# A graph-attention layer and a graph convolution on one core: new order of the first loads and products, adjacency transposed on VectorE, shorter sums and another order at the end

## The chip, the cores and the metric

The kernel runs on one core of one Trainium2 chip. The metric is the device time of one execution in microseconds (us). The numbers come from repeated executions and from one execution taken with the hardware profiler, whose trace has the start and the duration of every instruction. Times in the trace count from its first instruction; the time from there to the last one is called the span. An engine name in a profile line means: PE is TensorE (matrix products), PEld its loading of the stationary operand, DVE is VectorE, ACT is ScalarE, POOL is GpSimd, SP is SyncE (which here issues all loads and stores).

## The reference

There are 32 items x of 512 rows and 512 columns (fp32), one 512x512 adjacency of zeros and ones, three weights Wq, Wk, Wv with biases, and one weight W1 with bias b1.

```python
q, k, v = x @ Wq + bq, x @ Wk + bk, x @ Wv + bv          # 8 heads of 64
scores = einsum('bihd,bjhd->bhij', q, k) / 8 + where(adj == 0, -1e9, 0)
x = layernorm(x + softmax(scores) @ v)
y = einsum('nm,bmd->bnd', adj, x)
x = layernorm(x + y @ W1 + b1)
```

## The kernel before

**Products.** A product of two 512x512 matrices is made by seven products of 256x256 blocks instead of eight (a scheme of Strassen's kind). FACTORS (L53) names the two factors of each of them. Products 1 (A11 with B11) and 2 (A12 with B21) need plain blocks; the other five need sums and differences of blocks, such as S1 = A21 + A22, S2 = S1 - A11 and T1 = B12 - B11. A is the transposed item (tile xT, seven slots), B the weight (tiles wq, wk, wv, w, seven slots). The tile of a slot is overwritten where it can be: S3 takes the place of A21, T3 that of B12. `sum_weights` (L299) makes one sum of a weight on VectorE, `combine_rows` (L311) those of an item. `block_product` (L343) makes one of the seven, four matmuls into one of eight PSUM banks; since the data are fp32 the trace shows two records for each matmul, here called passes. `project` (L353) makes a product for q, k or v and adds it from the bank to its places.

**An item's way.** An item comes in as blocks or squares, and is transposed. q, k and v are made. The scores are products of k and q for a pair of heads at a time (L558); VectorE adds the mask (`gap`, one byte per element, 1 where the adjacency is zero) while it takes them out of PSUM (L560); ScalarE makes the exponentials (L562); GpSimd adds them up (L573); `attend` (L575) multiplies them with v (L582). `fold_squares` (L609) transposes the added exponentials in squares of 32, sums them, and sends the parts through HBM to their rows (`passed`, L626 and L633). `add_up` (L635) makes the sums and their reciprocals of a group of four heads, and also keeps running totals of both (`sums`, L639; `inverses`, L641), from which `judge` (L668) decides at the end whether the scheme was safe for these data; if not, a plain kernel would run. `scale_rows` and `add_rows` (L647, L654) add the attention to the item. Then come the layer norm (`statistics`, `square_root`, `invert_root`, `normalise`, L406 to L428), the splitting of each normalised item into a high part, exact in the faster matmul type, and the low rest (`split_high`, `split_low`, L430 to L443; L443 also adds b1 to the item on GpSimd), the product with the adjacency (`aggregate`, L462), the seven products with W1 (`convolve`, L513), the second norm and the store.

**Order.** The order is written out by hand; nothing reorders it. Each engine does its instructions in the order of the program. The items are staggered: while item b is in attention, b+1 is projected and b-1 aggregated and convolved. `units_of` (L756) lays these units between the products. Loads and stores all go through SyncE's queue in program order, with eight semaphores used in turn, so that a DMA waits until the one eight places before it has landed.

**The start.** L260 and L261 load item 0 in four blocks of 128 rows and Wq in two halves of its columns. `x_transpose` (L317) transposes a block by four matmuls with the identity into one bank; ScalarE copies the bank (L326), and for the two lower blocks VectorE adds S1 (L328). The first loads after that, from Wk on, wait for a small write to `wk` by ScalarE (L695) that stands behind the third block's copy. The adjacency is loaded whole (L700), and its four block rows are transposed on TensorE (L284) between products of k and v; `adjacency` (L281) then copies the bank (ScalarE, L285) and compares it (VectorE, L286).

**The end.** In the last group there are no more scores. `last_residual` (L658) transposes the attention of the last two pairs of heads on TensorE, multiplies by the reciprocals (L663) and adds to the last item (L665). Its norm, its splitting by rows (`split_rows`, L478) and its aggregation (`aggregate_rows`, L494, with 32 matmuls at L501) follow; beside them the item before it gets its seven products (`rest`), b1 is added (`add_bias`, L491), `judge` runs, and the last item's seven products (`last`) begin when L506 and L508 have copied the banks. The four 128-row blocks of the last item are normalised and stored one by one.

Of the kernel before, what the change touches and what calls it, by code (L numbers as in the profile page):

```python
# [207 lines left out]
def fast_kernel(ctx: ExitStack, tc, verdict, x, adj, Wq, bq, Wk, bk, Wv, bv, W1, b1, out):  # L208
# [28 lines left out]
    def load_blocks(b):  # L237

        for c in range(NB):
            IN[b, c] = work.tile([P, D], FP, name="xin", bufs=XIN)  # L240
            nc.sync.dma_start(IN[b, c], x[b, c * P:(c + 1) * P, :])

    def load_squares(b):


        for d in range(DB):
            IN[b, d] = work.tile([P, N // SQ, SQ], FP, name="xin", bufs=XIN)
            for i in range(P // SQ):
                cols = x[b, :, d * P + i * SQ:d * P + (i + 1) * SQ]
                nc.sync.dma_start(IN[b, d][i * SQ:(i + 1) * SQ, :, :], cols.rearrange("(j r) f -> r j f", r=SQ))  # L250
# [9 lines left out]
    load_blocks(0)  # L260
    wq = load_factors(Wq, "wq")  # L261
# [9 lines left out]
    sums = consts.tile([P, NB, GROUP], FP, name="sums")  # L271
    inverses = consts.tile([P, NB, GROUP], FP, name="inverses")
    nc.gpsimd.memset(sums, 0.0)
    nc.gpsimd.memset(inverses, 0.0)
# [6 lines left out]
    def adjacency(c):  # L281
        pt = bank(NB, P)
        for m in range(NB):
            nc.tensor.transpose(pt[:, m, :], adj_s[:, c, m * P:(m + 1) * P], ident)  # L284
        nc.scalar.activation(adjT[:, :, c * P:(c + 1) * P], pt, AF.Copy)  # L285
        nc.vector.tensor_scalar(gap[:, :, c * P:(c + 1) * P], pt, 0.0, None, op0=ALU.is_equal)  # L286

    def look_for_low_half(c):

        kept = work.tile([P, N], FR, name="high")  # L290
        nc.scalar.activation(kept, adj_s[:, c, :], AF.Copy)
        cut = work.tile([P, N], FP, name="attT")
        nc.vector.tensor_tensor(cut, adj_s[:, c, :], kept.bitcast(FP), op=ALU.not_equal)
# [23 lines left out]
    def x_transpose(b, c):  # L317

        if c == 0:
# [3 lines left out]
        for d in range(DB):  # L323
            nc.tensor.transpose(pt[:, d // 2, d % 2, :], IN[b, c][:, d * P:(d + 1) * P], ident)
        below, cols = c // 2, slice(c % 2 * P, (c % 2 + 1) * P)
        nc.scalar.activation(xt[:, 2 * below:2 * below + 2, :, cols], pt, AF.Copy)  # L326
# [16 lines left out]
    def block_product(pm, t, w, i, turned=False):  # L343
# [4 lines left out]
        for r in range(2):  # L348
# [4 lines left out]
    def project(b, which, i):  # L353
# [12 lines left out]
        pm = bank(2, half)  # L366
        block_product(pm, XT[b], w, i, turned=not values)
# [19 lines left out]
    def flips(b):  # L387

        return [(turn_squares if b else x_transpose, b, c) for c in range(NB)] + [(sum_rows, b)] if b < B else []
# [538 lines left out]
```

## Time and profile before

| What | us |
|---|---|
| median of three executions | 2744.57 (2743.18 to 2746.03) |
| profiled execution, its own time | 2743.55 |
| its span in the trace | 2741.7 |
| TensorE busy within the span | 2720.6 |
| VectorE, ScalarE, GpSimd busy | 2145.6, 1411.0, 1914.2 |
| first product with a weight begins | 8.30 |
| first scores begin | 38.34 |
| last product with a weight ends | 2729.53 |

A line of the timeline gives the start, the duration, the engine, the source line, the operation, what it writes and reads, the shape, and how many such instructions were merged; in brackets stands how long the engine was idle before it, and what ended that. The idle time of an engine costs something only if the engine, or one that waits for it, is what the end waits for.

### The profile page before, as it was taken

How to read it: one execution, taken by the hardware profiler on the slowest of the kernel's cores; microseconds unless marked ns; L12 is line 12 of the kernel's file. 1: busy time of each engine (PE TensorE's matmuls, PEld its weight loads, DVE VectorE, ACT ScalarE, POOL GpSimd, SP SyncE). 2: the span in 40 equal slices, each digit the busy share in tenths (PEclk: the TensorE clock that was granted, in tenths of full speed). 3: DMA queues.
4: the chain of work that ended last, by engine and by line, in shares of the span. 5: the costliest groups of instructions: out<-in, count | busy, mean ns of one | idle time of the engine just before them, and what ended most of it. 6: DMA issues, size and time to landing. Idle time of an engine off the chain costs nothing.

```text
span 2741.7 us, 36328 instructions
## 1 busy us (share of the span) xinstructions
PE 2720.6 (99%) x12344; PEld 1903.7 (69%) x12344; DVE 2145.6 (78%) x3540; ACT 1411.0 (51%) x2459; POOL 1914.2 (70%) x1221
## 2 busy tenths in 40 slices
PE   9999999999999999999999999999999999999997
PEld 6676676766766767667677676676776766767765
DVE  6878778788787787877877778778778787787787
ACT  3455464555544655545545455464465544655554
POOL 4776677766867667777677766686766867767774
PEclk9999999999999999999999999999999999999998
DMA  5223231233221332212323123331233222332121
GB/s 159 49 36 79 69 74 36 60 79 75 67 44 56 75 79 63 54 51 71 79 67 63 45 64 79 71 71 39 61 76 77 65 48 55 72 79 64 48 63 48
DMA packets 632927, 179.16 MB, mean 65 GB/s; under 512 B 578464, under 2 KB 582560, under 8 KB 632736
## 3 DMA queue, kind: packets, MB, share of 16 engines
q1 hardware_dynamic: 632736, 176.79, 27.3%
q8 instruction: 99, 1.62, 0.2%
q14 instruction: 92, 0.75, 0.1%
HBM read 108.01 MB, written 68.68 MB: 64 GB/s over the span
## 4 chain that ended last, share of the span: by engine, by line
PE 96%; DVE 2%; DMA 0%; ACT 0%; POOL 0%; issue 0%; SPq 0%; DVEq 0%; ACTq 0%
PE bank L350 56%; PE bank L558 17%; PE bank L582 16%; PE bank L469 8%; DVE bnst L412 0%; DVE e L560 0%; DMA wq<-in_L_gnn_Wq_dram 0%; DVE xs L531 0%; DVE xT L531 0%; DVE k L442 0%; POOL xs L529 0%; ACT xs L427 0%; DVE sums L639 0%; DVE stat L413 0%; DVE part L861 0%
## 5 line engine op out<-in xcount | busy, mean ns | idle before, releaser
L562 ACT ACTIVATE e<-e 128x1024 f32<-128x1024 f32 x512 | 524.9, 1053 | 575.2 <-DVE e L560 539.9
L573 POOL TENSOR_TENSOR es<-e 128x1024 f32<-128x1024 f32 x128 | 316.5, 2473 | 481.1 <-ACT e L562 481.1
L560 DVE SCALAR_TENSOR_TENSOR e<-gap,bank 128x512 f32<-128x512 uint8 x1024 | 617.7, 678 | 20.2 <-PE bank L558 20.2
L573 POOL TENSOR_TENSOR es<-es,e 128x1024 f32<-128x1024 f32 x256 | 618.9, 2418 | 20.1
L558 PE MATMUL bank<-q,k 64*128 64x512 f32 x2048 | 463.7, 598 | 0.0
L582 PE MATMUL bank<-e,v 128*64 128x512 f32 x2048 | 453.6, 595 | 0.0
L350 PE MATMUL bank<-wv,xT 128*128 128x256 f32 x1792 | 405.4, 381 | 0.0
L350 PE MATMUL bank<-xT,wk 128*128 128x256 f32 x1792 | 402.8, 379 | 0.0
L350 PE MATMUL bank<-xT,wq 128*128 128x256 f32 x1792 | 400.8, 381 | 1.2 <-DMA wq<-in_L_gnn_Wq_dram 1.0
L350 PE MATMUL bank<-w,yT 128*128 128x256 f32 x1792 | 392.6, 379 | 2.7 <-DVE yT L506 2.7
L350 PEld LDWEIGHTS bank<-wv,xT 128*128 128x128 f32 x1792 | 337.7, 190 | 70.2 <-DVE e L560 24.3
L350 PEld LDWEIGHTS bank<-xT,wq 128*128 128x128 f32 x1792 | 337.8, 190 | 69.9 <-DVE e L560 23.5
L558 PEld LDWEIGHTS bank<-q,k 64*128 64x128 f32 x2048 | 203.8, 186 | 258.3 <-issue 147.8
L350 PEld LDWEIGHTS bank<-w,yT 128*128 128x128 f32 x1792 | 340.1, 190 | 51.4 <-DVE yT L506 3.1
L350 PEld LDWEIGHTS bank<-xT,wk 128*128 128x128 f32 x1792 | 340.2, 190 | 46.1
L652 ACT ACTIVATE rows<-rows,zero,inverse 128x64 f32<-128x64 f32 x1008 | 343.1, 426 | 2.1 <-DVE inverse L640 2.1
L582 PEld LDWEIGHTS bank<-e,v 128*64 128x64 f32 x2048 | 141.3, 137 | 277.1 <-issue 275.7
L562 ACT ACT_TABLE_LOAD x30 | 38.5, 1283 | 406.1 <-DVE e L560 406.1
L442 DVE TENSOR_TENSOR low<-xs,high 128x512 fp32r<-128x512 f32 x122 | 163.1, 1337 | 61.5 <-ACT high L438 61.5
L531 DVE TENSOR_TENSOR xs<-bank,xs 128x512 f32<-128x512 f32 x186 | 124.3, 683 | 96.6 <-PE bank L350 57.2
L427 ACT ACTIVATE xs<-xs,shift,rstd 128x512 f32<-128x512 f32 x248 | 181.9, 803 | 32.0 <-DVE shift L422 21.3
L443 POOL TENSOR_TENSOR xs<-xs,b_r 128x512 f32<-128x512 f32 x124 | 157.4, 1282 | 21.5 <-DVE low L442 21.5
(125 smaller groups left out, 3013.0 us busy)
## 6 DMA issues: line engine op xcount, KB each, us to landing
turned<-attT SPq DMA_DIRECT2D x126, 256.0 KB, 2.0
rows<-turned SPq DMA_DIRECT2D x504, 64.0 KB, 2.5
xin<-in_x_dram SPq DMA_DIRECT2D x496, 64.0 KB, 2.4
xs<-in_x_dram SPq DMA_DIRECT2D x31, 1024.0 KB, 5.2
out_dram<-xs SPq DMA_DIRECT2D x31, 1024.0 KB, 4.4
part<-passed SPq DMA_DIRECT2D x256, 8.0 KB, 1.8
passed<-part SPq DMA_DIRECT2D x64, 32.0 KB, 1.5
xin<-in_x_dram SPq DMA_DIRECT2D x4, 256.0 KB, 3.2
```

The source lines that it names most:

```text
L350: nc.tensor.matmul(pm[:, r, :], left[:, d, r * P:(r + 1) * P], right[:, d, :], start=(d == 0), stop=(d == 1))
L427: nc.scalar.activation(row, row, AF.Identity, bias=SHIFT[t][:, slot:slot + 1], scale=RSTD[t][:, slot:slot + 1])
L442: nc.vector.tensor_sub(LOW[b, d], cols, HIGH[b, d].bitcast(FP))
L443: nc.gpsimd.tensor_add(cols, cols, b1_r[:, None, d * P:(d + 1) * P].to_broadcast([P, NB, P]))
L469: nc.tensor.matmul(pm.rearrange("p a n -> p (a n)"), part, adjT[:, n % NB, :], start=(n == 0), stop=(n == 2 * NB - 1))
L531: nc.vector.tensor_add(block, pm, block)
L558: nc.tensor.matmul(ps[s], keys[:, j * P:(j + 1) * P], queries, start=True, stop=True)
L560: nc.vector.scalar_tensor_tensor(e[:, s, :], gap[:, j, :], NEG * root, ps[s], op0=ALU.mult, op1=ALU.add)
L562: nc.scalar.activation(e, e, AF.Exp, scale=1.0 / root)
L573: nc.gpsimd.tensor_add(ES[b, hp], ES[b, hp] if j > 1 else E[b, hp, 0], E[b, hp, j])
L582: nc.tensor.matmul(po[s * HD:(s + 1) * HD, :], values, e[:, s, :], start=(j == 0), stop=(j == NB - 1))
L652: nc.scalar.activation(part, part, AF.Identity, bias=zero, scale=inverse[:, c, s:s + 1])
```

## The change

It has these parts.

1. Item 0 and Wq are loaded in smaller pieces in another order: left halves of the first two blocks, B11, their right halves, the two lower blocks, B21, B12, B22. TensorE transposes the left halves, makes half of product 1, transposes the right halves, makes the other half, transposes block 2 and block 3, and makes product 2, before the five products that need sums. What is added from the banks of products 1 and 2 keeps its place in the order of the adding.
2. The adjacency is loaded in 16 pieces, placed so that VectorE's transposition of 32x32 squares gives the transposed matrix. It is transposed there and not on TensorE. The 16 loads stand behind those of Wv and bv. ScalarE copies and VectorE compares the result from SBUF.
3. `add_up` keeps one running total of both sums and reciprocals, added by GpSimd in one instruction; VectorE's addition goes. `judge` takes one reduction in place of two and a minimum in place of two multiplications.
4. In the last group the second folding and the fetching of its parts come before the last two low parts. For the last item but one b1 is added by `add_bias` after the last item's statistics are issued, and no longer in `split_low`.
5. After the last group the last item's statistics come before the first of the `rest`; the second norm's statistics of the item two places before the last, and the biases of the last item, are laid between the products of `rest`. The last store but one and the last change places.

The numbers of rows and columns computed stay as they were. The core of the diff:

```diff
-    def load_blocks(b):
-        for c in range(NB):
+    def load_block(b, c, cols=slice(0, D)):
+        if (b, c) not in IN:
             IN[b, c] = work.tile([P, D], FP, name="xin", bufs=XIN)
-            nc.sync.dma_start(IN[b, c], x[b, c * P:(c + 1) * P, :])
+        nc.sync.dma_start(IN[b, c][:, cols], x[b, c * P:(c + 1) * P, cols])
...
+    def place_squares(t, rows, d):
+        for i in range(P // SQ):
+            cols = rows[:, d * P + i * SQ:d * P + (i + 1) * SQ]
+            nc.sync.dma_start(t[i * SQ:(i + 1) * SQ, :, :], cols.rearrange("(j r) f -> r j f", r=SQ))
...
-    load_blocks(0)
-    wq = load_factors(Wq, "wq")
+    for c in range(2):
+        load_block(0, c, slice(0, half))
+    load_factor("B11", 0, 0)
+    for c in range(2):
+        load_block(0, c, slice(half, D))
+    for c in (2, 3):
+        load_block(0, c)
+    for name, r, c in (("B21", 1, 0), ("B12", 0, 1), ("B22", 1, 1)):
+        load_factor(name, r, c)
...
     def adjacency(c):
-        pt = bank(NB, P)
-        for m in range(NB):
-            nc.tensor.transpose(pt[:, m, :], adj_s[:, c, m * P:(m + 1) * P], ident)
-        nc.scalar.activation(adjT[:, :, c * P:(c + 1) * P], pt, AF.Copy)
-        nc.vector.tensor_scalar(gap[:, :, c * P:(c + 1) * P], pt, 0.0, None, op0=ALU.is_equal)
+        turned = work.tile([P, N], FP, name="attT")
+        nc.vector.transpose(turned, adj_s[:, c, :, :].rearrange("p j f -> p (j f)"))
+        nc.scalar.activation(adjT[:, c, :], turned, AF.Copy)
+        nc.vector.tensor_scalar(gap[:, c, :], turned, 0.0, None, op0=ALU.is_equal)
...
-    def x_transpose(b, c):
+    def x_transpose(b, c, sides=(0, 1)):
...
-        for d in range(DB):
+        for d in (2 * s + k for s in sides for k in range(2)):
             nc.tensor.transpose(pt[:, d // 2, d % 2, :], IN[b, c][:, d * P:(d + 1) * P], ident)
...
-        nc.gpsimd.tensor_add(cols, cols, b1_r[:, None, d * P:(d + 1) * P].to_broadcast([P, NB, P]))
+        if b != B - 2:
+            nc.gpsimd.tensor_add(cols, cols, b1_r[:, None, d * P:(d + 1) * P].to_broadcast([P, NB, P]))
...
-        nc.vector.tensor_reduce(inverse, PART.pop((b, g)).rearrange("p a c h -> p c h a"), axis=AX.X, op=ALU.add)
-        nc.vector.tensor_add(sums, sums, inverse)
-        nc.vector.reciprocal(inverse, inverse)
-        nc.gpsimd.tensor_add(inverses, inverses, inverse)
+        nc.vector.tensor_reduce(total, PART.pop((b, g)).rearrange("p a c h -> p c h a"), axis=AX.X, op=ALU.add)
+        nc.vector.reciprocal(inverse, total)
+        nc.gpsimd.tensor_add(watched, watched, both)
...
-        nc.vector.tensor_reduce(seen[:, 0:1], sums, axis=AX.XY, op=ALU.add)
-        nc.vector.tensor_reduce(seen[:, 1:2], inverses, axis=AX.XY, op=ALU.add)
+        nc.vector.tensor_reduce(seen[:, 0:2], watched.rearrange("p k c h -> p k (c h)"), axis=AX.X, op=ALU.add)
...
-        nc.vector.tensor_mul(well[:, 0:1], well[:, 0:1], well[:, 1:2])
-        nc.vector.tensor_mul(well[:, 0:1], well[:, 0:1], well[:, 2:3])
+        nc.vector.tensor_reduce(well[:, 3:4], well[:, 0:3], axis=AX.X, op=ALU.min)
...
-    turned, first = flips(0), projections(0)
-    run(turned[:3])
+    first = projections(0)
+    for c in range(2):
+        x_transpose(0, c, (0,))
+    one, two = bank(2, half), bank(2, half)
+    block_product(one, XT[0], wq, 1, turned=True, parts=(0,))
+    for c in range(2):
+        x_transpose(0, c, (1,))
+    block_product(one, XT[0], wq, 1, turned=True, parts=(1,))
+    x_transpose(0, 2)
...
-    adj_s = work.tile([P, NB, N], FP, name="yT", bufs=1)
-    nc.sync.dma_start(adj_s, adj.rearrange("(c p) m -> p c m", p=P))
     wv = load_factors(Wv, "wv")
     bv_r = load_row(nc, consts, bv, "bv_r")
+    adj_s = work.tile([P, NB, N // SQ, SQ], FP, name="yT", bufs=1)
+    for c in range(NB):
+        place_squares(adj_s[:, c, :, :], adj, c)
...
-    run(turned[3:NB])
+    x_transpose(0, 3)
+    block_product(two, XT[0], wq, 2, turned=True)
...
-    run(first[:1])
+    project(0, "q", 1, one)
...
-    run(first[3:5])
+    run(first[3:4])
+    project(0, "q", 2, two)
...
-            behind = [fresh[:2], fresh[2:], young[:1] + scaled[:1], young[1:3], young[3:5] + [first],
-                      young[5:] + splits[:1], splits[1:] + scaled[1:]]
-            return [merge(convolution(b - 2), behind), [second] + fetched + added + gathered]
+            behind = [fresh[:2], fresh[2:], young[:1] + scaled[:1], young[1:3], young[3:5] + [first],
+                      young[5:] + splits[:1], splits[1:2] + [second] + fetched + splits[2:] + scaled[1:]]
+            return [merge(convolution(b - 2), behind), added + gathered]
...
-    run(rest[:1])
     for c in range(NB):
         statistics(t, 0, c)
+    for c in range(NB):
+        add_bias(t - 1, c)
+    run(rest[:1])
     ahead = norm(t, 0)
     run(ahead[:1] + rest[1:2] + ahead[1:2])
+    older, seen = survey(t - 2), survey(t - 1)
     for c in range(NB):
         run(ahead[2 + c:3 + c])
         split_rows(t, c)
+        if c == 0:
+            add_bias(t, c)
+        if c == 2:
+            run(older[:2])
         run(rest[2 + c:3 + c])
-    run(rest[2 + NB:])
-    older, seen = survey(t - 2), survey(t - 1)
-    run(older)
-    for c in range(NB):
-        add_bias(t, c)
+        if c > 0:
+            add_bias(t, c)
+    run(rest[2 + NB:] + older[2:])
     well = judge()
...
-    store(t, [2, 3])
+    store(t, [3, 2])
```

## The prediction

> **What bounds the kernel now.** I read the page's busy table and chain first, then TensorE's waits, then the windows and the timeline at both ends.
>
> ```profile
> PE 2720.6 (99%) x12344; PEld 1903.7 (69%) x12344; DVE 2145.6 (78%) x3540; ACT 1411.0 (51%) x2459; POOL 1914.2 (70%) x1221
> PE 96%; DVE 2%; DMA 0%; ACT 0%; POOL 0%; issue 0%; SPq 0%; DVEq 0%; ACTq 0%
> ```
>
> TensorE is busy in 2720.6 of 2741.7 us. So between the ends nothing but fewer products can help, and the diff leaves those products alone. VectorE work saved there (63 of the 64 additions of L639) is worth nothing. What can be won lies in the 21.1 us in which TensorE is idle, in products that go, and in stretches where it runs slowly. Its waits, in total, times, longest:
>
> ```profile
> PE bank L501 <- DVE low L489: 3.2, 1, 3.2
> PE bank L350 <- DVE yT L506: 2.7, 1, 2.7
> PE bank L690 <- DVE attT L687: 1.1, 1, 1.1
> PE bank L350 <- DMA wq<-in_L_gnn_Wq_dram: 1.0, 1, 1.0
> ```
>
> Two waits are in the last 40 us, two at the start; 12.2 us more lie behind the last product (2729.53 to 2741.7). The windows of TensorE (start:end, length, busy, granted clock, DMA) show a cost that no wait shows:
>
> ```profile
> 2700.00:2704.00 4.00, 0.76 (x4) 0.85 0.00 0
> 2704.00:2708.00 4.00, 4.00 (x10) 0.50 0.01 4
> 2708.00:2712.00 4.00, 4.00 (x15) 0.80 0.00 0
> ```
>
> After the 3.24 us of idling the clock falls to half: L501's products follow each other every 0.43 us until 2709.5, and every 0.24 us after. Two timeline stretches, VectorE at the end and the first products:
>
> ```profile
> 2692.18 0.26 DVE L638 TENSOR_REDUCE inverse<-part 128x16 f32<-128x64 f32 x1 [3.50 <-DMA part<-passed]
> 2692.47 1.09 DVE L639 TENSOR_TENSOR sums<-sums,inverse 128x16 f32<-128x16 f32 x1
> ...
> 2714.24 1.18 DVE L676 TENSOR_TENSOR well<-well 128x1 f32<-128x1 f32 x1
> 2715.45 1.19 DVE L677 TENSOR_TENSOR well<-well 128x1 f32<-128x1 f32 x1
> ```
>
> ```profile
> 7.99 0.42 DVE L328 TENSOR_TENSOR xT<-bank,xT 128x256 f32<-128x256 f32 x1 [0.20 <-ACT xT L326]
> 8.30 1.97 PE L350 MATMUL bank<-xT,wq 128*128 128x256 f32 x8 [0.97 <-DMA wq<-in_L_gnn_Wq_dram]
> 9.75 0.69 DVE L302 TENSOR_TENSOR wq<-wq 128x512 f32<-128x512 f32 x1 [1.33 <-DMA wq<-in_L_gnn_Wq_dram]
> 10.49 7.17 PE L350 MATMUL bank<-xT,wq 128*128 128x256 f32 x32 [0.23 <-DVE wq L302]
> 24.41 0.60 PE L284 MATMUL bank<-ident,yT 128*128 128x128 f32 x4
> ```
>
> A multiplication of one element per partition (L676) takes 1.18 us, on the path to L506 for which TensorE waits.
>
> **What the skill says.** "SBUF — State Buffer", Who interferes with whom: a VectorE instruction with two SBUF inputs and a GpSimd one that reads SBUF exclude each other for the whole instruction. The trace agrees: L676 and L677 end at 2715.42 and 2716.64, near the boundaries of GpSimd's four L492 of 1.24 us each (2711.65 to 2716.62). The same section says that tensor_reduce never contends; L670 to L672 took about 0.15 us beside a running L492. "TensorE: Matmul & The Clock Gate", Part 1: after an idle window of about 3.4 us the clock is halved, and the window runs freely, so the moment varies. The trace agrees with 3.24 us here, while the wait of 2.72 us left the clock at 1.00.
>
> **The start.** All times are on the trace's clock. The data are the same 2 MB; the four x blocks and Wq landed from about 4.0 to 9.7 us, some 0.83 us per 256 KB. By the new order I estimate the two left halves landed by 4.0, B11 by 4.9, right halves 5.7, block 2 by 6.5, block 3 by 7.3, B21 8.1, B12 9.0, B22 9.8. SyncE issues ten instead of six DMAs at 0.45 us, the last near 5.3, so it isn't the limit.
> - Left transposes: 4.21 to 5.06 (0.213 each, half clock as now). Two copies on ScalarE at 4.88 and 5.31; the first half of product 1 starts at 5.83. The clock rose near 6.4 in this trace: two passes at 0.43, two at 0.216, end 7.12.
> - Right transposes to 7.55 (0.108 each), second half of product 1 to 8.41, block 2 to 8.84, block 3 to 9.27, product 2 (eight passes, 1.73) to 11.0.
> - The next product (5) needs S1 and T1. ScalarE copies block 2 at 9.04 and block 3 at 9.66 (its 0.6, and L695 between); VectorE's two L328 end at 10.1 and 10.7, T1 at 11.3, product 5 at 11.37. Today it starts at 10.49: 0.88 later, but product 2 is done: **-0.85**.
> - The new waits: VectorE's T1 queues behind L328 of block 3, with product 5 behind it. The load of Wk waits for L695, now 9.7 instead of 7.23, with all of SyncE's later loads behind it. Wk lands by about 15; its first product is due at 16.5, so this costs nothing. The bank of product 2 stays occupied longer, but the order built from the changed kernel gives it to no product before v's first.
> - The 16 transposes of the adjacency (L284) leave TensorE: from 24.41 to 31.34 are 6.93 us, less three products of 1.73: **-1.75**. Their work goes to VectorE: four transposes at 0.62 (L335's price for 128x512) and four comparisons from SBUF of 0.3 to 0.7, in place of four of 0.68. VectorE has gaps over 1 us between its instructions there.
> - The adjacency now comes in 16 DMAs of 128-byte pieces. Sixteen such loads of x took 14.2 us of SyncE beside other loads (13.57) and 8.7 us alone (77.96). I take 10 us behind Wk, Wv and bv (18.8): last landing 28.8, needed at about 31.2; VectorE can be some 3 us late before the scores (35.7) wait. The loads of x behind them move to about 39, wanted at 56. Cost 0.
>
> **The end.**
> - The second folding moves ahead of the last two low halves (L442). With the bias additions (L443) gone from GpSimd, L442 d=1 runs 2680.2 to 2680.9 (now 1.40), the fold until 2683.3 instead of 2687.45. The part's store and fetch take 4.7 us, so it lands at 2688.1 instead of 2692.2. Low half d=2 is made at 2683.5 to 2684.2, if the lock alternates as now; TensorE wants it at 2683.68. **+0.6** on TensorE (up to 1.9 if both L656 go first); its seven products with W1 for the last item but one then end at about 2701.2 instead of 2700.55.
> - add_up starts after L474 at about 2689.2: reduction 0.29, reciprocal 0.36, no L639, then the four of L663/L665 (2.68) to 2692.55, four statistics (3.2) to 2695.75. GpSimd's four biases stand at 2693.3 to 2698.3. L531 of product 1 waits for two of them (2695.85). L422 has two SBUF inputs: it may be blocked until 2698.3. I take that; unblocked it is 1.0 earlier. ScalarE's normalisation at 2698.45, the first low row at 2700.6 (L427 to PE now takes 2.34). So TensorE has no wait: L501 starts at about 2701.2, at full clock.
> - L501: 32 at 0.235 are 7.5 us; the fourth low row, which I find blocked by GpSimd until 2706.35, costs 0.3: end about 2709.0 instead of 2713.98.
> - VectorE then: two L531, two statistics (2709.7), two reductions, a tensor_scalar that waits for GpSimd (2710.8; L674 did so, 0.55), two short ones: L506 at 2711.1 instead of 2716.56. Products resume at 2711.85 instead of 2717.30: **-5.45**. GpSimd is free by 2712.1, and its L315 starts at about 2713.2.
> - From there the order is the same, until the last stores: block 3 goes out when ready (2735.24), block 2 at 2735.7; today the last is issued at 2736.14: **-0.4**.
> - The middle: **0**. `watched` takes the place of the addition to `inverses` on GpSimd (0.22 for 16 elements; 32 are now added), under a TensorE that never pauses; without that cover, twice 0.22 in 64 groups would cost 14 us at most.
>
> Sum: -0.85 - 1.75 - 5.45 - 0.4 = -8.45. The span goes from 2741.7 to 2733.25, the profiled execution (2743.55) to 2735.1. That execution is 1.02 under the median 2744.57, so I forecast 2736.1.
>
> **Rivals.**
> 1. The front gives nothing. TensorE's work now starts while the clock may still be half; if it rises at 8 instead of 6.4, product 5 is 1.3 later, and the S1 chain hides nothing. Today slack before 8.30 swallows that. Worth 2.1 less: 2738.2. Against it: in this trace the clock had risen by 6.66.
> 2. The locks fall well: L422 and the tensor_scalar aren't blocked, 2 us better: 2734.1.
> 3. The locks fall badly, or the clock halves again while TensorE waits for L506 (2.2 us by my times, under the 2.72 that did no harm). Eight products' passes at half speed for some 3 us and one more block of 1.25: about 3.4 less: 2739.5.
> 4. Slower: the adjacency's small pieces come late. The first scores need its last comparison, 3.1 us after the landing. They start at 38.34 today; break-even (with 5.85 won at the end) is a landing at 41. If the 16 loads take 29 us (1.8 each, twice what the busiest stretch shows), landing is at 48 and the time 2744.57 - 8.45 + 15.4 = 2751.5. The 0.89 seen when crowded gives 33, within slack.
>
> **Chances.** Forecast 0.50, rival 1 0.20, rival 2 0.14, rival 3 0.12, rival 4 0.04. 0.2% (5.5 us) is about what a measurement of this kernel can tell from no change. Faster than 2739.1: the forecast, rival 2, most of rival 1, a little of rival 3: 0.79. Within: 0.16. Slower: 0.05. The range spans rivals 2 to 3, with 1.5 us for the spread of the runs: 2732.6 to 2740.0.
>
> **What would show it.** L284 gone from TensorE; product 5 near 11.4 with product 2 ahead of it; scores near 35.7. TensorE's wait at L501 under 0.5 us and PEclk at 1.0 in 2700 to 2712; add_up near 2689; L506 near 2711; the last product ending near 2721.5 (now 2729.5, less 8.05 of start and end). Wrong if scores wait for VectorE's comparison, if the clock still falls at the end, or if the first sums are ready much after 11.4.

## The result, and the profile after

| What | before, us | after, us |
|---|---|---|
| median | 2744.57 (2743.18 to 2746.49) | 2732.80 (2731.98 to 2734.13) |
| profiled execution: its time, its span | 2743.55, 2741.7 | 2731.98, 2730.2 |
| TensorE, VectorE busy | 2720.6, 2145.6 | 2716.4, 2103.9 |
| k's first product begins | 17.50 | 15.89 |
| first scores begin | 38.34 | 34.98 |
| first scores to the last attend (L582, now L600) | 2633.63 | 2633.23 |
| last attend to the first VectorE copy of the last aggregation (L506, now L524) | 44.59 | 37.39 |
| that copy to the end of the last ScalarE operation (L427, now L444) | 19.12 | 19.20 |
| from there to the end of the span | 6.0 | 5.4 |

The ratio is 0.9957, with a 95% interval of 0.9944 to 0.9970: 11.8 us less, where 8.5 were forecast (2736.1; range 2732.6 to 2740.0). The stretches of the table add up along the path: -3.36 - 0.40 - 7.20 + 0.08 - 0.6 = -11.5, the difference of the spans.

The page's busy line and the engines' shares of its chain of waits, of the kernel after:

```profile
PE 2716.4 (99%) x12328; PEld 1900.3 (70%) x12328; DVE 2103.9 (77%) x3478; ACT 1410.8 (52%) x2461; POOL 1913.8 (70%) x1220
PE 97%; DVE 1%; POOL 0%; DMA 0%; ACT 0%; issue 0%; SPq 0%; DVEq 0%; ACTq 0%; POOLq 0%
```

TensorE has 16 passes fewer, and still bounds all but the ends. Its waits after (us in total, times, longest):

```profile
PE bank L365 <- DVE yT L524: 1.9, 1, 1.9
PE bank L707 <- DVE attT L704: 1.1, 1, 1.1
PE bank L365 <- ACT xT L341: 0.5, 1, 0.5
PE bank L487 <- DVE k L459: 0.2, 1, 0.2
```

The 3.2 us ahead of the last aggregation are gone, those for L506 are 1.9 instead of 2.7, the 1.0 for Wq at the start is gone. The windows of TensorE at the end (start:end, length, busy, clock, DMA):

```profile
2700.00:2704.00 4.00, 4.00 (x18) 1.00 0.00 0
2704.00:2708.00 4.00, 2.08 (x9) 0.95 0.00 0
2708.00:2712.00 4.00, 4.00 (x13) 0.63 0.00 0
```

The last aggregation now runs at full clock. But the clock falls later, behind the 1.92 us of waiting for L524: 38 of the last item's 56 passes took 10.15 us, and before it was 8.47:

```profile
2717.30 8.47 PE L350 MATMUL bank<-w,yT 128*128 128x256 f32 x38 [2.72 <-DVE yT L506]
```

The stretch from L524 to the end of the last ScalarE operation grew by only 0.08. That is the first thing to explain. VectorE's timeline after, at the places shown of before (add_up, and judge with the first copy):

```profile
2684.08 0.42 DVE L492 TENSOR_TENSOR yT<-bank,yT 128x256 f32<-128x256 f32 x1 [1.45 <-ACT yT L490]
2684.42 0.25 DVE L657 TENSOR_REDUCE inverse<-part 128x16 f32<-128x64 f32 x1
2684.70 0.25 DVE L658 RECIPROCAL inverse<-inverse 128x16 f32<-128x16 f32 x1
...
2692.71 0.73 DVE L439 SCALAR_TENSOR_TENSOR shift<-stat,rstd 128x4 f32<-128x4 f32 x1
2695.03 0.69 DVE L507 TENSOR_TENSOR low<-xT,high 128x512 fp32r<-128x512 f32 x1 [1.59 <-ACT high L506]
...
2704.70 0.73 DVE L692 TENSOR_SCALAR well<-seen 128x2 f32<-128x2 f32 x1
2705.35 0.14 DVE L693 TENSOR_SCALAR well<-seen 128x1 f32<-128x1 f32 x1
2705.53 0.16 DVE L694 TENSOR_REDUCE well<-well 128x1 f32<-128x3 f32 x1
2705.60 0.68 DVE L524 COPY yT<-bank 128x512 f32<-128x512 f32 x1
```

add_up no longer waits for its parts (3.50 us before); it stands behind L492, which waits for the aggregation itself. From L507 to L524 VectorE has no gap. The first products after:

```profile
5.35 1.13 PE L365 MATMUL bank<-xT,wq 128*128 128x256 f32 x4 [0.53 <-ACT xT L341]
6.32 0.60 PE L339 MATMUL bank<-ident,xin 128*128 128x128 f32 x4
6.75 1.03 PE L365 MATMUL bank<-xT,wq 128*128 128x256 f32 x4
7.62 1.04 PE L339 MATMUL bank<-ident,xin 128*128 128x128 f32 x8
8.81 7.25 PE L365 MATMUL bank<-xT,wq 128*128 128x256 f32 x32
15.89 3.62 PE L365 MATMUL bank<-xT,wk 128*128 128x256 f32 x16
```

Product 2 is the first quarter of the 32 passes at 8.81. It ends at about 10.6, and product 5, whose sum T1 is made by VectorE from 9.81 to 10.49, follows without a gap.

### The profile page after: what moved, and what is told of

It reads as the page before. It is cut to its first block, busy times and chain, and to the rows that moved or that the text cites. A ratio compares the mean times of both kernels' runs of the same rounds, so it can differ in the third digit from the quotient of the medians.

```text
span 2730.2 us, 36268 instructions
## 1 busy us (share of the span) xinstructions
PE 2716.4 (99%) x12328; PEld 1900.3 (70%) x12328; DVE 2103.9 (77%) x3478; ACT 1410.8 (52%) x2461; POOL 1913.8 (70%) x1220
## 4 chain that ended last, share of the span: by engine, by line
PE 97%; DVE 1%; POOL 0%; DMA 0%; ACT 0%; issue 0%; SPq 0%; DVEq 0%; ACTq 0%; POOLq 0%
PE bank L365 56%; PE bank L576 17%; PE bank L600 16%; PE bank L487 8%; POOL es L591 0%; DVE xs L549 0%; DVE bnst L429 0%; DVE e L578 0%; DMA wq<-in_L_gnn_Wq_dram 0%; DVE part L639 0%; SPq L241 0%; DVE v L637 0%; DVE part L896 0%; DVE mix L545 0%; DVE k L459 0%
## 5 line engine op out<-in xcount | busy, mean ns | idle before, releaser
L600 PE MATMUL bank<-e,v 128*64 128x512 f32 x2048 | 453.6, 595 | 0.0
L600 PEld LDWEIGHTS bank<-e,v 128*64 128x64 f32 x2048 | 141.3, 137 | 277.1 <-issue 275.1
L444 ACT ACTIVATE xs<-xs,shift,rstd 128x512 f32<-128x512 f32 x248 | 181.9, 803 | 27.1 <-DVE shift L439 17.7
L490 ACT ACTIVATE yT<-bank 128x512 f32<-128x512 f32 x124 | 74.2, 598 | 186.8 <-PE bank L487 186.8
```

The source lines that it names most:

```text
L444: nc.scalar.activation(row, row, AF.Identity, bias=SHIFT[t][:, slot:slot + 1], scale=RSTD[t][:, slot:slot + 1])
L490: nc.scalar.activation(yt[:, d // 2:d // 2 + 3:2, d % 2, :], pm, AF.Copy)
L600: nc.tensor.matmul(po[s * HD:(s + 1) * HD, :], values, e[:, s, :], start=(j == 0), stop=(j == NB - 1))
```

## The experiments

My theory after the result: at the end VectorE's queue sets the time, and TensorE's pauses and clock there hardly count. At the start two independent sums are saved. The rivals were the clock, and single parts of the change. Each kernel was timed beside the kernel before, whose medians were 2744.49 to 2745.00. In the table, positions are from the profiled executions. "Attend to copy" is the path through the end that VectorE's chain makes, "wait" is TensorE's longest wait between the last aggregation and the last product, and "half" says that passes at half clock follow it.

| Kernel | median | first scores | scores to attend | attend to add_up | attend to first low row | attend to copy | attend to last ScalarE end | wait |
|---|---|---|---|---|---|---|---|---|
| before | 2744.57 | 38.34 | 2633.63 | 20.21 | 30.98 | 44.59 | 63.71 | 2.72 |
| after | 2732.80 | 34.98 | 2633.23 | 16.21 | 26.82 | 37.39 | 56.59 | 1.92, half |
| e1 start only | 2740.97 | 35.32 | 2633.99 | 19.85 | 30.69 | 44.26 | 63.46 | 3.77, half |
| e2 end only | 2736.30 | 39.14 | 2633.11 | 16.20 | 26.81 | 37.39 | 56.52 | 1.93 |
| e3 adjacency on TensorE | 2734.92 | 37.26 | 2633.15 | 16.17 | 26.79 | 37.36 | 56.56 | 1.92, half |
| e4 product 2 late | 2735.44 | 38.85 | 2633.22 | 16.19 | 26.81 | 37.38 | 56.58 | 1.93, half |
| e5 sums on VectorE | 2734.37 | 35.53 | 2633.85 | 16.79 | 28.06 | 38.63 | 57.77 | 1.92 |
| e6 fold late | 2734.02 | 35.98 | 2633.24 | 17.39 | 27.46 | 38.03 | 57.17 | 1.93 |
| e7 judge multiplies | 2734.94 | 35.59 | 2633.40 | 16.20 | 26.82 | 38.53 | 57.73 | 3.08, half |
| e8 before, clock kept | 2744.83 | 38.33 | 2633.59 | 20.27 | 30.97 | 44.56 | 64.91 | 3.49, half |
| e9 biases by columns | 2731.81 | 35.67 | 2633.27 | 15.78 | 25.82 | 36.40 | 55.54 | 1.50 |
| e10 judge later | 2733.22 | 35.32 | 2633.35 | 16.18 | 26.80 | 36.30 | 57.96 | 2.5, half |
| e11 copies on ScalarE too | 2732.50 | 35.63 | 2633.35 | 16.19 | 26.80 | none | 56.74 | 2.4, half |
| e12 combined | 2729.05 | 35.36 | 2633.35 | 15.77 | 25.82 | none | 53.22 | none |

The nine executions with the changed start begin the scores at 34.98 to 35.98 (median 35.53), the three with the old one at 38.33 to 39.14 (median 38.34). Two things vary from run to run there. Loads land at other times. And the clock rises at another moment, 4.22 to 7.00 us in the nine: in order of that rise, the nine also start their scores in order, from 34.98 (after) to 35.98 (e6). The two that rise at 4.22 and 4.23 (after, e10) still lie 0.35 apart. Positions behind the attend repeat within about 0.05 where the code of the end is the same, so they are the finer reading; medians less than 1 us apart are not told apart.

**e1 and e2: the halves.** Of the diff, e1 holds what bears on loads, `x_transpose`, `block_product`, `project`, `adjacency` and the schedule of the start; e2 holds the rest (`watched`, `add_up`, `judge`, the fold's place, biases, the last items, the store order).

> The kernel before with the changes of the start alone (loads by halves and blocks, products 1 and 2 between the transposes, adjacency turned by VectorE). Theory: what the start wins is carried unchanged through the middle, since TensorE never pauses there, and is independent of the end. The first scores start at 35.0 (before 38.3), the last attend starts 3.4 earlier than before, the stretch from there to the first copy of the last aggregation stays at 44.6 us, and the time is about 2741.2. Rival A: slack further on swallows the start: scores at 35.0 but the time within 0.5 of 2744.6. Rival B: the end's stalls depend on when the end is reached: the stretch of 44.6 us changes by over 1 us.

> The kernel before with the changes of the end alone (fold earlier, statistics ahead of the first product, biases moved, shorter judge, one addition of the sums fewer on VectorE, order of the last two stores). Theory: the stretch from the last attend to the first copy of the last aggregation falls from 44.6 to 37.4, the part behind the last ScalarE operation from 6.0 to 5.4; time about 2736.5, and the two halves together give the whole (3.4 + 8.1). Rival A: half of the end's gain came from being reached at another time: about 2740. Rival B: the middle gains too, by the 63 additions that VectorE no longer makes: the middle shorter by over 1 us, time under 2735.

Measured: 2740.97 (ratio 0.9987, 0.9981 to 0.9994) and 2736.30 (0.9970, 0.9958 to 0.9982), 3.5 and 8.2 less than before: together 11.7, the whole. The theory held on the whole: the start is carried through the middle, and up to the copy e2's end equals after's within 0.02 at every position. Two of its details missed: in e1's trace the last attend came 2.7 earlier instead of 3.4, and in e2's the part behind the last ScalarE operation took 5.7 instead of 5.4. These two also bear on the clock of the last products, since one ran them at half speed and one at full, without any edit for that. Timeline of TensorE, e1 and then e2:

```profile
2714.30 10.16 PE L367 MATMUL bank<-w,yT 128*128 128x256 f32 x38 [3.77 <-DVE yT L525]
```

```profile
2710.38 8.47 PE L348 MATMUL bank<-w,yT 128*128 128x256 f32 x38 [1.93 <-DVE yT L505]
```

From the copy to the last ScalarE operation e1 took 19.20 and e2 19.13. 1.7 us of slower products cost 0.07 there. Six kernels whose program is the same from the copy on show it again, and show why: behind the copy comes VectorE's shift (L439 of the kernel after), which GpSimd's additions block there. At half clock (after, e3, e4) it began 4.03 to 4.36 behind the copy and took 0.23 to 0.56; at full clock (e2, e5, e6) it began 3.84 or 3.85 behind it and took 0.76. In all six it ended 4.59 to 4.61 behind the copy, where GpSimd's second addition after the copies (L330) ends.

**e3: the adjacency back on TensorE**, loaded in one piece:

```
-        turned = work.tile([P, N], FP, name="attT")
-        nc.vector.transpose(turned, adj_s[:, c, :, :].rearrange("p j f -> p (j f)"))
+        pt = bank(NB, P)
+        for m in range(NB):
+            nc.tensor.transpose(pt[:, m, :], adj_s[:, c, m * P:(m + 1) * P], ident)
...
```

> The changed kernel with the adjacency loaded in one piece and turned by TensorE again. Theory: 16 transposes come back on an engine that doesn't wait there, so the first scores start 1.75 later (36.7) and the time is about 2734.5. Rival: TensorE waits near them anyway, or the scores wait for VectorE's comparison: scores within 0.5 of 35.0, time 2732.8.

Measured 2734.92, with TensorE's timeline:

```profile
23.32 1.89 PE L365 MATMUL bank<-xT,wk 128*128 128x256 f32 x8
25.05 0.60 PE L299 MATMUL bank<-ident,yT 128*128 128x128 f32 x4
25.49 1.89 PE L365 MATMUL bank<-xT,wk 128*128 128x256 f32 x8
```

k's first product to the scores takes 20.84 us, as before, against 19.09 after: 1.75, four times the 0.44 between a group of four transposes and what follows it. The forecast's term is exact.

**e4: product 2 in its old place**, loads and halves as changed:

```
-    block_product(two, XT[0], wq, 2, turned=True)
...
-    run(first[3:4])
-    project(0, "q", 2, two)
+    run(first[3:5])
```

> The changed kernel with product 2 made after product 7 as before, loads and product 1 as changed. Theory: the first product with a sum (5) is bound by its sums and starts near 10.5 with or without product 2 ahead of it, so product 2 costs its own 1.73 later: k's first product at 17.6, scores at 36.7, time about 2734.5. Rival: the earlier sums, by the order of loads, are what won: without product 2 in the way the sums' products start near 8.8 and the time stays at 2732.8.

Measured 2735.44. The sums were not early, so the rival fell. But the cost is more than product 2's 1.73: the scores came at 38.85. The timeline, and the windows of TensorE in the same kernel:

```profile
11.09 8.83 PE L365 MATMUL bank<-xT,wq 128*128 128x256 f32 x32 [1.83 <-DVE wq L317]
```

```profile
10.00:12.00 2.00, 0.91 (x3) 0.83 0.74 170
12.00:14.00 2.00, 2.00 (x6) 0.50 0.91 313
14.00:16.00 2.00, 2.00 (x9) 0.82 0.86 244
```

The hole of 1.83 us in which product 2 otherwise lies let the clock fall, and 32 passes took 8.83 instead of some 7.15. So product 2 ahead of the sums fills a wait of its own size, and it covers the clock as well in such an execution.

**e5: the addition to the sums back on VectorE** (two accumulators, three reductions in `judge`):

```
-        nc.vector.reciprocal(inverse, total)
-        nc.gpsimd.tensor_add(watched, watched, both)
+        nc.vector.tensor_add(sums, sums, inverse)
+        nc.vector.reciprocal(inverse, inverse)
+        nc.gpsimd.tensor_add(inverses, inverses, inverse)
...
```

> The changed kernel with the addition to the sums back on VectorE in every group (two accumulators, three reductions at the end). Theory: at the two ends it costs what it is blocked for, since VectorE's chain sets the time there: the aggregation after the last attend starts about 0.8 later (7.8 behind the attend instead of 7.0), the last add_up is about 1.1 longer, the first copy of the last aggregation comes about 1.9 later behind the attend (39.3 instead of 37.4); in the middle the first scores to the last attend take about 0.5 more (2633.7). Time about 2735.2. Rival, the prediction's step: only the last of the 64 counts: middle and aggregation as they are, 1.1 in all, 2733.9.

Measured 2734.37. In its timeline of VectorE the addition in the last group but one and in the last:

```profile
2665.03 1.77 DVE L659 TENSOR_TENSOR sums<-sums,inverse 128x16 f32<-128x16 f32 x1
...
2686.45 1.18 DVE L659 TENSOR_TENSOR sums<-sums,inverse 128x16 f32<-128x16 f32 x1
```

The first makes the low half d=0 1.73 later behind the attend (6.71 instead of 4.98), and TensorE waits for it: the aggregation starts 7.54 behind the attend instead of 7.02. The copy comes 1.24 later; I had expected 1.9, but the shift (L441) now misses GpSimd's biases and takes 0.16. So the rival's "only the last of the 64 counts" fell: add_up, which lies ahead of the last addition, is 0.58 later already. The theory's mechanism stands at two thirds of its size, and in time the result (2734.37) lies nearer to the rival's 2733.9 than to its 2735.2. In the middle the four executions with this addition took 2633.59 to 2633.99, the ten without 2633.11 to 2633.40: about 0.5 in all for the other 62, by a way that was not traced.

**e6: the second fold behind the last low halves again:**

```
-                      young[5:] + splits[:1], splits[1:2] + [second] + fetched + splits[2:] + scaled[1:]]
-            return [merge(convolution(b - 2), behind), added + gathered]
+                      young[5:] + splits[:1], splits[1:] + scaled[1:]]
+            return [merge(convolution(b - 2), behind), [second] + fetched + added + gathered]
```

> The changed kernel with the second folding and the fetch of its parts behind the last low halves, as before. Theory: the parts land about 3.2 later behind the attend, and the whole chain of VectorE with them: first copy of the last aggregation at about 40.6 behind the attend instead of 37.4, or up to 43 if the longer wait of TensorE ahead of the last aggregation halves its clock and it is then the one that is late; the aggregation gives 0.4 back. Time 2735.5 to 2738. Rival: the biases and the shorter judge made the gain, and the parts have slack: under 0.7, 2733.5 at most.

Measured 2734.02, copy 0.64 later: the rival's bound, and the theory's 3.2 fell. The reduction of add_up in this kernel's timeline:

```profile
2686.61 0.26 DVE L657 TENSOR_REDUCE inverse<-part 128x16 f32<-128x64 f32 x1 [1.54 <-DMA part<-passed]
```

The parts land 17.39 behind the attend, only 1.2 after the place at which add_up goes in the changed kernel, where it stands behind L492 and not behind the parts. In the kernel before the fold was later still, since its low halves began 2.0 later and the first two were further apart. The earlier fold is thus worth 1.2 at add_up and 0.6 at the copy once the other edits are made.

**e7: the judge's two multiplications** in place of the minimum:

```
-        nc.vector.tensor_reduce(well[:, 3:4], well[:, 0:3], axis=AX.X, op=ALU.min)
+        nc.vector.tensor_mul(well[:, 0:1], well[:, 0:1], well[:, 1:2])
+        nc.vector.tensor_mul(well[:, 0:1], well[:, 0:1], well[:, 2:3])
...
```

> The changed kernel with the two multiplications of one element per partition in place of the minimum in the judge. Theory: VectorE's chain sets the end, and GpSimd is adding biases then: the two are blocked again and the first copy of the last aggregation comes 1.5 to 2.2 later (39 to 39.6 behind the attend), the last ScalarE operation as much later; time 2734.3 to 2735. Rival A: they fall behind GpSimd's last bias and cost 0.3 in all: 2733.1. Rival B: what TensorE's clock does after the longer wait (4 us) counts as well: 1.7 more, 2736.5.

Measured 2734.94. The two of them on VectorE:

```profile
2706.24 1.18 DVE L694 TENSOR_TENSOR well<-well 128x1 f32<-128x1 f32 x1
2707.45 0.16 DVE L695 TENSOR_TENSOR well<-well 128x1 f32<-128x1 f32 x1
```

One was blocked and one not, as GpSimd's last addition there ends between them: the copy comes 1.14 later, less than the 1.5 to 2.2 expected, and so does the last ScalarE operation (57.73 instead of 56.59). TensorE's longer wait (3.08) costs nothing more.

**e8: the kernel before with its clock kept.** 24 unneeded products are put ahead of the last aggregation:

```
         banks = [bank(2, half) for _ in range(DB)]
+        for _ in range(24):
+            nc.tensor.matmul(banks[0][:, 0, 0:P], ident, ident, start=True, stop=True)
```

> The kernel before with 24 products of the identity with itself in TensorE's idle time ahead of the last aggregation, so that its clock isn't halved there. It adds work that isn't needed and changes no result. Theory: the last aggregation's 32 products run at full speed and end about 2.4 earlier, but VectorE's judge holds the copies: first copy at 44.6 behind the attend as before, time 2744.5 within 0.5. Rival: the half clock was on the path and its end is what won the 2.4: first copy at about 42.2, time about 2742.1.

Measured 2744.83 (ratio 0.9999, 0.9990 to 1.0007). TensorE's timeline of this kernel:

```profile
2700.30 5.52 PE L499 MATMUL bank<-ident 128*128 128x128 f32 x48
2705.58 0.48 PE L503 MATMUL bank<-adjT,low 128*128 128x512 f32 x1
...
2713.13 0.59 PE L350 MATMUL bank<-w,yT 128*128 128x256 f32 x2
```

The edit overshot: each fp32 product is two passes, so the 24 took 5.28 us and the aggregation began 1.8 later, then ran at full clock and ended 0.85 earlier (2713.13, before 2713.98), not 2.4. Still the copy stands at 44.56, as before (44.59), so none of the 0.85 arrives. The rival that the half clock was the price of the end fell. One surprise: from the copy to the last ScalarE operation it took 1.2 longer. The clock fell again behind the 3.49 us wait, VectorE's L422 came at 2721.17, and GpSimd's third L315 had just taken over (boundaries at about 2721.04 and 2722.28):

```profile
2721.17 1.13 DVE L422 SCALAR_TENSOR_TENSOR shift<-stat,rstd 128x4 f32<-128x4 f32 x1
```

In e1 the same instruction came 0.16 ahead of such a boundary, took 0.18, and the half clock cost nothing:

```profile
2717.97 0.18 DVE L441 SCALAR_TENSOR_TENSOR shift<-stat,rstd 128x4 f32<-128x4 f32 x1
```

GpSimd's instructions of 1.24 us thus swallow a delay of a few tenths, or make 1.2 of it. This is the rule of the Trainium skill's "SBUF — State Buffer", Who interferes with whom, that issue order decides who blocks; here it shows as 0.18 against 1.13 for the same [128x4] operation.

**e9: the biases by columns as before**, so `b != B - 2` of `split_low` and the four `add_bias(t - 1, c)` are taken out:

> The changed kernel with the biases of the last item but one added column by column behind each low half, as before, instead of row by row behind the last item's statistics. Theory: the four additions on GpSimd (1.25 each) fall among VectorE's low halves, which have two SBUF inputs, and put off the residual and the sums on GpSimd behind them: first copy of the last aggregation 1 to 2 later (38.4 to 39.4 behind the attend), time 2733.8 to 2734.8. Rival A: they are hidden, and the gain there is the fold's and the judge's: 37.4, 2732.8. Rival B: without them, VectorE's last shift and the second addition of the first product are free of GpSimd: 0.6 to 1.4 earlier (36 to 36.8), 2731.4 to 2732.2.

Measured 2731.81, the copy at 36.40: rival B held, and my theory had the wrong sign. The changed kernel's way of adding these biases loses 1.0 us. The shift in this kernel:

```profile
2693.00 0.16 DVE L439 SCALAR_TENSOR_TENSOR shift<-stat,rstd 128x4 f32<-128x4 f32 x1
```

It isn't blocked (0.16 instead of 0.73), add_up stands 0.43 earlier, and low halves d=2 and 3 took 1.29 for the two instead of 2.42: they fall into a pause of GpSimd, and not beside its residual (L675).

**e10 and e11: the judge behind the third of the last seven products; in e11 also all four copies on ScalarE.**

```
-    well = judge()
     aggregate_rows(t)
...
+        if unit[2] == 5:
+            well = judge()
...
-            if d % 2:
-                nc.vector.tensor_copy(block, pm)
-            else:
-                nc.scalar.activation(block, pm, AF.Copy)
+            nc.scalar.activation(block, pm, AF.Copy)
```

> The changed kernel with the judge moved from ahead of the last aggregation's copies to behind the third of the last seven products, where VectorE waits for others now and then and GpSimd is idle. Theory: the copies start 1.1 us earlier (36.3 behind the attend), and the judge costs there what VectorE has too little of gaps for, 0.6 or so: last ScalarE operation 0.3 to 0.9 earlier behind the attend than in the changed kernel (56.6), time 2732.2. Rival: VectorE is busy without a gap from there to the end, so the judge costs in one place what it saves in the other: no difference, 2732.8.

> As the one with the judge later, and all four copies of the last aggregation on ScalarE instead of two on VectorE. Theory: VectorE sets the end, so taking 1.2 us of copies and the judge from its chain there lets TensorE go on almost without a wait (under 0.7 us instead of 1.9) with its clock kept, and then TensorE's 56 products (13.2) set the end: last ScalarE operation 2 to 3 earlier behind the attend than in the changed kernel (53.6 to 54.6 instead of 56.6), time 2730 to 2731. Rival: GpSimd's three sums (3.7 us) behind the last of these copies bind as they do now: under 1 us, 2732.

Measured 2733.22 and 2732.50: no gain, and neither theory nor rivals had the reason. Waits and windows of TensorE in e11:

```profile
PE bank L920 <- DVE well L691: 2.4, 1, 2.4
```

```profile
2712.00:2716.00 4.00, 1.63 (x10) 1.00 0.69 262
2716.00:2720.00 4.00, 4.00 (x11) 0.57 0.68 260
```

L920 is TensorE's small product for the verdict, queued ahead of products 3 and 4. With the judge later it waits for VectorE, which is behind TensorE there; both products queue behind it, and then run at half clock (16 passes in 5.40, otherwise 3.72). The copies were indeed earlier (36.30 in e10), and the new wait took it back. Two of e10's five executions (2731.84, 2731.87) and one of e11's (2730.90) are 1.3 us or more below the others of their kernel, about what a fall of the clock costs; whether these kept their clock is not known, as the traces are of other executions.

**e12: both, without that wait, and with e9.** The verdict's product goes behind the last of the seven; the judge behind product 7's additions, its comparison made one element at a time:

```
-        nc.vector.tensor_scalar(well[:, 0:2], seen[:, 0:2], BOUND, None, op0=ALU.is_le)
+        for k in range(2):
+            nc.vector.tensor_scalar(well[:, k:k + 1], seen[:, k:k + 1], BOUND, None, op0=ALU.is_le)
...
```

> Four edits on the changed kernel together: biases of the last item but one by columns as before; all four copies of the last aggregation on ScalarE; the judge behind VectorE's two additions of product 7, its comparison of two elements per partition made as two of one element; TensorE's product for the verdict behind the last of the seven products, so that nothing of TensorE's waits for the judge. Theory: the run with the judge later and the copies on ScalarE lost its gain to one new wait, TensorE's 2.4 for the judge, and to the half clock after it; without that wait VectorE's two additions of product 7 come 1.5 earlier behind the attend than in the changed kernel's and the chain behind them keeps its 8.3: last ScalarE operation at 53.3 to 54.3 behind the attend (changed kernel 56.6, the biases alone 55.5), time 2729.8 to 2730.8. Rival: GpSimd's sums and the additions behind product 7 bind there, whatever stands ahead of them: 55.5, time 2731.8 as with the biases alone.

Measured 2729.05 (2728.75 to 2729.47), ratio to before 0.9942 (0.9928 to 0.9956): 3.75 under the changed kernel. The last ScalarE operation ends 53.22 behind the attend, just ahead of the theory's 53.3 to 54.3. Apart from the biases (e9), how the gain divides among the edits was not tested. TensorE no longer stops after the last aggregation:

```profile
2703.75 12.25 PE L365 MATMUL bank<-w,yT 128*128 128x256 f32 x56
2715.93 0.19 PE L917 MATMUL bank<-ones,well 128*1 128x1 f32 x2
```

## Why the prediction was right, and where it wasn't

- **Start, -0.85 and -1.75.** By the two profiled executions it was -1.61 and -1.75. By the medians of nine and three executions the scores came 2.81 earlier against 2.60 forecast, so most of the excess in the first term is the scatter of the start. The argument that product 2 lies in the wait for T1 was right (e4); T1 ended at 10.49, not 11.3: in this execution the clock had risen at 4.22, earlier than the 6.4 that I took, and the copies of half a bank took 0.38 each. That the pieces of the adjacency cost nothing was right: nothing waits for them.
- **Middle, 0.** It gave 0.4 to 0.5. The step that failed is that VectorE work saved between the ends, "63 of the 64 additions of L639", is worth nothing. The addition in the last group but one stands just ahead of the last attend, and took 1.78 us:

```profile
2667.62 1.78 DVE L639 TENSOR_TENSOR sums<-sums,inverse 128x16 f32<-128x16 f32 x1
```

  The low halves began 2.0 earlier behind the attend without it (e5 gives 1.73 of that back). TensorE, which had idled 0.75 for them, starts its aggregation 7.02 behind the attend instead of 7.84 (in e5 7.54).
- **End, -5.45; measured -7.20.** By the chain, add_up was forecast at 17.2 behind the attend and measured at 16.21. It stands behind that aggregation, which starts 0.82 earlier and which the later low half d=2 held up by 0.4, not 0.6. From add_up to the first low row made, 11.4 were forecast and 11.30 measured (2684.42 to 2695.72). So the lock on L422 (L439 after) was right too: I took it as blocked until the biases ended, and it ends at 2693.44, with GpSimd's four biases at 2693.42:

```profile
2688.47 4.95 POOL L510 TENSOR_TENSOR xs<-xs,b_r 128x512 f32<-128x512 f32 x4
```

  From that low row to the copy, 10.5 were forecast and 9.88 measured. The excess lies behind the fourth low row, where VectorE's additions, statistics and judge took 3.81 instead of 4.75, with the judge's tensor_scalar blocked (0.73) as forecast. So the two terms that were mis-sized are add_up's place and this last stretch of VectorE. Of the first, e5 gives back 0.58 with the additions; where the other 0.4 comes from was not separated.
- **The clock.** I forecast full speed from 2700 to 2712. It held for the last aggregation and failed behind the wait for L524. Rival 3 named this and priced it as a loss; e1 beside e2 show 1.7 us on TensorE and 0.07 at the end. Both the fall and its small price are luck: of six such waits of 1.92 or 1.93 us three were followed by half clock (the last section shows on what it depends), and GpSimd's boundary happened to swallow the delay, as it did not in e8. And the recovery of the 2.4 us at L501, which looks like a gain of this change in the windows, was none: e8 ends that aggregation earlier and the copy doesn't move.
- **Stores, -0.4.** The end behind the last ScalarE operation took 6.0, 5.2 and 5.7 in the three kernels with the old order (before, e1, e8) and 5.0 to 5.8 in the others. The medians differ by 0.3, within the scatter; this term is open.
- **Rivals.** 4 didn't come, and 1 not in this execution; its mechanism shows in e6, where the clock rose at 7.00 and product 5 began at 11.63, 1.0 later than after. 2 (locks that fall well, 2734.1) came nearest in time, but by accident: L422 and the tensor_scalar were both blocked. The range's upper end should have been 2741.0 by its own rule (2739.5 and 1.5), not 2740.0; nothing rests on it.

In sum the direction and the parts were right, but 3.3 of the 11.8 us were not forecast, and the measured time lies only 0.2 inside the early end of the range. The end was undersized by 1.75, through two terms of the VectorE queue. What stays open: the path by which 62 additions make 0.5 in the middle, and the store order.

## What to carry to other kernels

When an engine's wait ends with another engine's copy, read that other engine's queue back to where it last had a gap; its whole content up to there is the price, and the waiting engine's own pauses and clock may be free. They need not be: the same half clock that cost 0.07 here cost 1.2 in e8, where it carried one instruction past a boundary. Moving an operation off that queue pays only if every instruction that consumes it moves too: one small product left in TensorE's queue took back all that e10 and e11 had won. And a tiny two-input operation on VectorE is to be priced by what GpSimd runs at that moment, not by its size.

## What the runs showed of the hardware

- **The clock changes on a grid of its own, and falls when enough waiting lies in one step of it.** In each of the 14 traces all changes of the granted clock lie whole multiples of 3.41 us apart (after: down at 2707.58, up at 2710.99; before: down at 2702.81, up at 2709.64). Cut into these steps, full speed was lost after each one in which TensorE was busy for 1.49 us or less, and kept after each with 1.68 or more; between them, 1.54 was followed by half clock (e4, at the start) and 1.52 was not (before, the wait of 2.72). So the length of a wait does not decide alone. Of the waits of 1.92 and 1.93 in six kernels, three were followed by half clock (after, e3, e4) and three not (e2, e5, e6). In the kernel after the wait lies in one step; in e2 it spans two. The windows of TensorE, cut at the steps, first after, then e2:

```profile
2704.17:2707.58 3.41, 1.49 (x8) 1.00 0.00 0
2707.58:2710.99 3.41, 3.41 (x10) 0.50 0.00 0
```

```profile
2706.57:2709.98 3.41, 1.88 (x9) 1.00 0.00 0
2709.98:2713.40 3.42, 3.02 (x14) 1.00 0.00 0
```

  Waits of 1.83 (e4, start), 2.4, 2.5, 3.08, 3.24, 3.49 and 3.77 were followed by half clock, those of 0.81 and 1.50 were not. "TensorE: Matmul & The Clock Gate", Part 1, gives an idle window of about 3.4 us that runs freely; length and free running agree with these steps, but a step needn't be idle throughout: up to 1.49 us of work in it did not save the clock, so the measurement decides. A step at half clock cost TensorE about 1.7 us (10.15 instead of 8.47 for 38 passes).
- **A comparison of [128x2] is blocked by GpSimd and one of [128x1] isn't.** 0.73 against 0.14 side by side in the kernel after (L692, L693). In e10 the same [128x2] took 0.17 while GpSimd ran nothing. In e12, made as two of one element, the two took 0.21 together at 2715.31, in the middle of three additions of GpSimd that run without a gap from 2714.47 to 2718.19. The lines of e10 and e12:

```profile
2716.08 0.17 DVE L692 TENSOR_SCALAR well<-seen 128x2 f32<-128x2 f32 x1
```

```profile
2715.31 0.21 DVE L689 TENSOR_SCALAR well<-seen 128x1 f32<-128x1 f32 x2
```

  "SBUF — State Buffer", Who interferes with whom, says that tensor_scalar can take the shared port pair in some of its forms; the runs show that two elements do and one does not.
